# Seven steps moved in a hand-written order: two layers of graph network on one Trainium2 core

## The chip, the cores and the metric

The kernel runs on one core of one Trainium2 chip. The metric is the time of one execution on the device, in microseconds (us); less is better. A core has TensorE (PE, with its weight loads as a row of their own, PEld), VectorE (DVE), ScalarE (ACT), GpSimd (POOL) and SyncE (SP). Each has its own queue of instructions and they wait for each other on semaphores. In this kernel ACT, SP and POOL also issue the transfers.

## The reference

x holds 128 samples of 128 nodes with 512 features, adj is one 128x128 matrix for all samples. Two layers follow each other, each with its residual:

```python
h = jnp.maximum(_layernorm(x, axis=-1), 0.0)
x = x + _L0_gnn_ref(h, adj, Wq, Wk, Wv)      # layer 0
h = jnp.maximum(_layernorm(x, axis=-1), 0.0)
x = x + _L1_gnn_ref(h, adj, Wq, bq, Wk, bk, Wv, bv)   # layer 1
```

Layer 0 has no softmax. With q, k, v = h Wq^T, h Wk^T, h Wv^T it computes

```python
rel = adjacency.T[None, :, :] * (q @ k.T)
rel = rel / jnp.linalg.norm(rel, axis=2, keepdims=True)
out = rel @ v
```

Layer 1 is attention with 8 heads of 64: scores q k^T / 8, minus 1e9 where adj is 0, softmax over the last axis, times v. Everything is float32.

## The kernel before

The samples go through in 32 groups of four. Layer 0 of a group is an object `m`, layer 1 of the group before it `l`, layer 1 of the one before that `p`. The layer 1 that is being prepared for the next cycle is `n`, the layer 0 that is being prepared is `f`. A cycle of the loop runs a list of steps, `name.step` or `name.product.step`, in the order in which a string lists them (L657 to L689): FIRST in cycle 0, SECOND in cycle 1, ORDER in cycles 2 to 31, LAST at the end. The last cycle of ORDER has no `f`, and steps of a missing object are left out. The order holds for each engine: what a step gives to DVE stands in DVE's queue in the order of the list, and so for PE, ACT, POOL and SP. Between engines only data and buffers make anyone wait.

Big products (512x512 by 512 features) are made by a scheme with seven half-size products in place of eight: class `Product`, steps P1 P2 P5 P6 P3 P7 P4 in that order of issue. Each step is eight matmuls of 128x256 on PE (L229) into a PSUM bank. There are three banks to a product: x is used by P1, P6, P7, P4, which add onto it in turn, y by P2, z by P5 and P3. In between, a copy of the bank is kept (`keep`, an ACT copy, but for V of layer 1 a DVE addition with the bias, L246), and a later step's bank is added to the kept copy on DVE (L253). So P6 may write x only after P1's copy has read it, P7 after P6's copy, and P4 after P7's addition. Four banks are shared by all products (`ps_mm`). The products are G and V in layer 0 (tile names pg and pv), Q, K and V in layer 1 (pq, pk, pv). P5 and P6 read sums of the turned input, made by `sumA` and `sumB` (two DVE additions each).

The steps around the change:

- `stat b`, `inv i`: mean and variance of sample b on DVE (L294, L295); for samples 2i and 2i+1 rstd and shift on POOL (four small operations, L301 to L304).
- `hn i`, `rd i`, `T i`: normalisation and relu of two samples on ACT (L312), which then sends them to DRAM (d_h); SP fetches them in four blocks in another layout (u_h); DVE turns 32x32 blocks (L324). T0 gives the half x11, x12 of the input, T1 the half x21, x22. The tile `u` has two buffers, shared with `wr`.
- `R`, `mask_rel`, `square`, `N`, `norms`: layer 0's q k^T (32 matmuls, L393, bank pr), masked on DVE (L402), squared on ACT, summed on PE (L420) and taken to the power -1/2 on POOL.
- `O b`, `xO b`: rel times v on PE (L433), the residual on DVE (L439). O2 and O3 read what P4 of V gave.
- `S b`, `mk`/`mkA`/`mkB`/`add_mask`/`mx`: layer 1's scores (L471), mask and maximum on DVE.
- `ex`/`exC`/`exD`, `wr b`, `wt b`: the exponentials on ACT, sent to DRAM (d_w); SP's fetch (u_w); `wt` takes the reciprocal of the sums (L508) and turns the exponentials on DVE (L510).
- `A i`, `oc i`, `rdo i`, `ot i`: weights times v, and the way out.
- `start`: makes the tiles and products, and issues nothing.
- `w.sumk`, `w.sumq`: four additions each on the weights, on DVE.

S of sample 1 takes its two PSUM banks from `ps_o` (two buffers), which also holds pr of R and the results of O and A. The four fetch issues of `rd`, `wr` and `rdo` stand in SP's queue in the order of the list.

Of the kernel before, what the change touches and what calls it, by code (L numbers as in the profile page):

```python
# [21 lines left out]
def kernel(  # L22
# [354 lines left out]
    class Layer0(Layer):  # L377
        n = 0
# [62 lines left out]
    class Layer1(Layer):  # L441
        n = 1
# [215 lines left out]
        m.sumA m.sumB m.start f.stat0 f.stat1 f.inv0 m.G.P1 m.G.P2 f.stat2 f.stat3 f.inv1 w.sumw m.G.P5 f.hn0 f.rd0 m.G.P6  # L658
        w.scale m.G.P3 m.V.P1 f.hn1 f.rd1 w.sumv w.loadx m.G.P7 m.V.P2 w.sumq m.G.P4 m.V.P5
        m.R m.mask_rel m.square f.T0 m.V.P6 m.V.P3 m.N m.norms m.V.P7 m.O0 m.xO0 m.O1 m.xO1 n.stat0 n.stat1  # L660
        n.inv0 m.V.P4 n.hn0 n.rd0 f.T1 m.O2 m.xO2 m.O3 m.xO3 n.stat2 n.stat3 n.inv1 f.sumA f.start f.G.P1
        f.G.P2 f.sumB w.sumk f.G.P5 n.hn1 n.rd1 f.G.P6 f.G.P3 f.G.P7 n.T0 f.G.P4 n.T1 n.start
    """.split()
    SECOND = """
        l.Q.P1 l.sumA l.Q.P2 l.sumB l.K.P1 l.K.P2 l.Q.P5 l.Q.P6 f.load0 f.load1 l.Q.P3 l.K.P5 l.K.P6 l.Q.P7
        l.K.P3 l.K.P7 l.S0 l.mk0 f.load2 f.load3 l.Q.P4 l.K.P4 l.ex0 l.wr0 m.V.P1 f.stat0 f.stat1 f.inv0
        m.V.P2 m.V.P5 l.wt0 m.R m.mask_rel m.square f.stat2 f.stat3 f.inv1 m.V.P6 l.S1 m.N l.S2 l.mkA1 m.norms l.exC1
        l.mkB1 l.exD1 l.wr1 m.V.P3 l.add_mask2 m.V.P7 l.mx2 l.exC2 m.O0 m.xO0 m.O1 m.xO1 n.stat0 n.stat1 n.inv0
        m.V.P4 l.exD2 l.wr2 n.hn0 n.rd0 l.start_v l.V.P1 m.O2 m.xO2 m.O3 m.xO3 n.stat2 n.stat3 n.inv1 l.V.P2 l.V.P5
        l.wt1 n.hn1 l.V.P6 l.wt2  # L670
        n.rd1 l.V.P3 l.V.P7 n.T0 l.S3 l.A0 l.mk3 l.oc0 l.V.P4 l.ex3 n.T1 n.start
# [6 lines left out]
        l.wt0 f.load2 f.load3 m.R m.mask_rel m.square m.V.P6 l.S1 m.N l.S2 l.mkA1 m.norms l.exC1 l.mkB1 l.exD1  # L678
        l.wr1 m.V.P3 l.add_mask2 m.V.P7 l.mx2 l.exC2 m.O0 m.xO0 m.O1 m.xO1 n.stat0 n.stat1 n.inv0 m.V.P4 l.exD2
        l.wr2 n.hn0 n.rd0 l.start_v f.stat2 l.V.P1 m.O2 m.xO2 m.O3 m.xO3 n.stat2 n.stat3 n.inv1 l.V.P2 l.V.P5 l.wt1  # L680
        f.stat3 f.inv1 n.hn1 l.V.P6 l.wt2
        n.rd1 l.V.P3 l.V.P7 n.T0 l.S3 l.A0 l.mk3 l.oc0 l.V.P4 l.ex3 n.T1 n.start
    """.split()
    LAST = """
# [19 lines left out]
    with tc.manual_schedule(engines={EN.PE, EN.SP, EN.Pool, EN.DVE, EN.Activation}):  # L704
        p, l, m = None, None, Layer0(0)
# [9 lines left out]
        f = Layer0(1)  # L715
# [3 lines left out]
        for g in range(NG):  # L719
            n = Layer1(g)  # L720
            if g:
                f = Layer0(g + 1) if g + 1 < NG else None
            run((FIRST, SECOND, ORDER)[min(g, 2)], p=p, l=l, m=m, n=n, f=f, w=Weights1())
            p, l, m = l, n, f
# [31 lines left out]
```

## Time and profile before

| | |
|---|---|
| median of 3 runs | 2506.55 us (2505.88 to 2507.48) |
| the profiled execution | 2507.47 us, span of its instructions 2505.7 us |
| mean granted TensorE clock | 0.998 |
| one ordinary cycle, from R to R | 76.73 us in most |
| POOL busy | 531.5 us (21%) |
| transfers | 405.72 MB, mean 162 GB/s |

A page of the profile gives busy time for each engine and the chain of work that ended last. Finer views used below: the timeline, one row for a run of equal instructions (start, duration, engine, line, operation, output<-inputs, shape, count) with, in brackets, how long the engine was idle before it and who released it; the sums over stretches (windows); and the waits by who waited for whom. Starts are counted from the first instruction. The end of a matmul is modelled, so distances are taken from start to start.

### The profile page before, as it was taken

The page shows a single profiled execution, that of the slowest core. Times are in us where ns is not written, and L with a number is a line of the kernel's source. Part 1 is how long each engine was busy: PE and PEld are TensorE (multiplying, and loading weights), DVE is VectorE, ACT ScalarE, POOL GpSimd, SP SyncE. Part 2 cuts the span into 40 slices and gives each one's busy share as a digit, 9 for nine tenths or more (in the row PEclk, how much of TensorE's full clock was granted, in tenths as well). Part 3 has the DMA queues.
Part 4 walks back from the last instruction along what each step waited for, and adds up shares of the span by engine and source line. Part 5 has one row for each costly group of instructions (what it writes and reads, how often), then busy time and mean ns, then how long its engine had stood idle before and what let it go on. Part 6 is the DMA issues. An engine that isn't in the chain of part 4 may idle for free.

```text
span 2505.7 us, 40908 instructions
## 1 busy us (share of the span) xinstructions
PE 2488.6 (99%) x14688; PEld 2114.5 (84%) x14688; DVE 1716.3 (68%) x2547; ACT 1024.3 (41%) x3248; POOL 531.5 (21%) x944
## 2 busy tenths in 40 slices
PE   9999999999999999999999999999999999999998
PEld 7788888888888888888888888888888888888887
DVE  6467766667766677666677666776667776667766
ACT  3334434344434444343434344443434443444433
POOL 5011212212221212122121211221221212112211
PEclk9999999999999999999999999999999999999999
DMA  6155644555544555455564455554455644455543
GB/s 207 60 169 168 189 142 156 162 177 177 161 153 153 178 164 190 139 159 169 168 185 156 155 152 179 166 184 145 151 169 169 193 147 153 155 177 177 166 137 118
DMA packets 370476, 405.72 MB, mean 162 GB/s; under 512 B 29601, under 2 KB 286753, under 8 KB 370273
## 3 DMA queue, kind: packets, MB, share of 16 engines
q1 hardware_dynamic: 279520, 168.97, 25.3%
q10 hardware_dynamic: 69856, 165.70, 17.6%
q0 software_dynamic: 20896, 68.44, 8.3%
q8 instruction: 116, 1.90, 0.3%
q14 instruction: 88, 0.71, 0.1%
HBM read 204.80 MB, written 198.18 MB: 161 GB/s over the span
## 4 chain that ended last, share of the span: by engine, by line
PE 95%; DMA 2%; DVE 1%; ACT 1%; issue 0%; SPq 0%; POOL 0%; ACTq 0%; DVEq 0%; POOLq 0%
PE pv_x L229 17%; PE pg_x L229 9%; PE pv_z L229 9%; PE pk_x L229 8%; PE pq_x L229 8%; PE pg_z L229 5%; PE pq_z L229 4%; PE po L616 4%; PE pr L393 4%; PE pk_z L229 4%; PE po L433 4%; PE pv_y L229 4%; PE pss L471 4%; PE pg_y L229 2%; PE pk_y L229 2%; PE pq_y L229 2%
## 5 line engine op out<-in xcount | busy, mean ns | idle before, releaser
L651 POOL TENSOR_TENSOR xb<-xb,o 128x512 f32<-128x512 f32 x124 | 158.0, 1274 | 1205.6 <-DVE o L644 1204.1
L229 PE MATMUL pv_x<-wc_v,h 128*128 128x256 f32 x1280 | 303.8, 384 | 0.0
L229 PEld LDWEIGHTS pv_x<-wc_v,h 128*128 128x128 f32 x1280 | 238.0, 190 | 58.6 <-issue 20.8
L229 PE MATMUL pv_z<-wc_v,s 128*128 128x256 f32 x1024 | 245.9, 383 | 0.0
L312 ACT ACTIVATE hn<-xb,shift,rstd 128x512 f32<-128x512 f32 x252 | 191.0, 807 | 127.0 <-POOL shift L304 124.8
L324 DVE STREAM_TRANSPOSE h<-u_h 128x1024 f32<-128x1024 f32 x126 | 156.1, 1239 | 107.1 <-DMA u_h<-d_h 106.9
L229 PEld LDWEIGHTS pv_z<-wc_v,s 128*128 128x128 f32 x1024 | 192.6, 190 | 28.9 <-issue 0.2
L495 ACT ACTIVATE e<-pss,nmax 128x128 f32<-128x128 f32 x512 | 179.9, 381 | 89.5 <-DVE nmax L488 75.0
L627 ACT COPY oT<-po 128x512 f32<-128x512 f32 x124 | 72.6, 586 | 274.1 <-PE po L616 274.1
L229 PE MATMUL pq_x<-h,wc_q 128*128 128x256 f32 x768 | 181.8, 380 | 0.9 <-DVE h L324 0.8
L229 PE MATMUL pv_x<-wc_v,s 128*128 128x256 f32 x768 | 181.7, 379 | 0.0
L229 PE MATMUL pk_x<-h,wc_k 128*128 128x256 f32 x768 | 181.5, 379 | 0.0
L294 DVE BATCH_NORM_STATS2 st<-xb 128x6 f32<-128x512 f32 x256 | 170.8, 667 | 8.4 <-DMA xb<-in_x_dram 8.4
L510 DVE STREAM_TRANSPOSE wT<-u_w 128x1024 f32<-128x1024 f32 x126 | 153.4, 1218 | 21.0 <-DMA u_w<-d_w 18.4
L229 PEld LDWEIGHTS pq_x<-h,wc_q 128*128 128x128 f32 x768 | 145.4, 190 | 22.1 <-PE pv_x L229 2.0
L229 PEld LDWEIGHTS pk_x<-h,wc_k 128*128 128x128 f32 x768 | 145.8, 190 | 19.9
L229 PEld LDWEIGHTS pv_x<-wc_v,s 128*128 128x128 f32 x768 | 143.3, 190 | 18.4 <-issue 0.2
L644 DVE TENSOR_TENSOR o<-o,rs 128x512 f32<-128x512 f32 x124 | 124.4, 1003 | 4.3
L229 PE MATMUL pg_z<-s,wc_a 128*128 128x256 f32 x512 | 124.1, 385 | 0.0
L301 POOL TENSOR_SCALAR rstd<-mv 128x2 f32<-128x2 f32 x128 | 28.4, 222 | 447.5 <-DVE mv L295 445.2
L616 PE MATMUL po<-wT,v 128*64 128x128 f32 x1984 | 122.0, 276 | 0.0
L229 PE MATMUL pq_z<-s,wc_q 128*128 128x256 f32 x512 | 121.6, 380 | 0.3
(157 smaller groups left out, 4834.5 us busy)
## 6 DMA issues: line engine op xcount, KB each, us to landing
d_h<-hn ACTq DMA_DIRECT2D x126, 512.0 KB, 3.6
u_h<-d_h SPq DMA_DIRECT2D x504, 128.0 KB, 3.5
d_w<-e ACTq DMA_DIRECT2D x126, 512.0 KB, 2.7
u_w<-d_w SPq DMA_DIRECT2D x504, 128.0 KB, 3.2
xb<-in_x_dram POOLq DMA_DIRECT2D x124, 256.0 KB, 3.1
d_o<-oT ACTq DMA_DIRECT2D x62, 512.0 KB, 3.0
u_o<-d_o SPq DMA_DIRECT2D x248, 128.0 KB, 2.9
out_dram<-xb POOLq DMA_DIRECT2D x124, 256.0 KB, 3.0
```

Of the source, the lines that this page charges most:

```text
L229: nc.tensor.matmul(ps[:, m, :], lhsT=lhsT, rhs=rhs, start=first and m == 0 and k == 0, stop=k == 1, skip_group_check=True,)
L294: nc.vector.bn_stats(st, x_tiles[g, b])
L312: nc.scalar.activation(hn[:, r], x_tiles[g, b].rearrange("p (k j q) -> p j k q", j=TB, q=BK), AF.Relu, bias=self.shift[:, b : b + 1], scal ...
L324: nc.vector.transpose(half.rearrange("p k (t i) -> p t k i", i=BK), self.u.pop(i).rearrange("p t (k q) -> p t k q", q=BK),)
L393: nc.tensor.matmul(pr[:, b, :], lhsT=self.turned(k, b), rhs=self.gT[:, k, ts(b, P)], start=(k == 0), stop=(k == KD - 1),)
L433: nc.tensor.matmul(po, lhsT=self.rel[:, b, :], rhs=self.v[:, b, :], start=True, stop=True)
L471: nc.tensor.matmul(half[r][:, k, :], lhsT=self.qT[rows, k, ts(b, P)], rhs=self.kT[rows, k, ts(b, P)], start=True, stop=True,)
L495: nc.scalar.activation(e[:, :, i, :], sc[:, i, :].rearrange("p (j q) -> p j q", q=BK), AF.Exp, bias=nmax[:, i : i + 1], accum_out=self.tot ...
L510: nc.vector.transpose(self.wT[b].rearrange("p h (t i) -> p t h i", i=BK), self.uw.pop(b).rearrange("p t (h q) -> p t h q", q=BK),)
L616: nc.tensor.matmul(po[r * HD : (r + 1) * HD, k, :], lhsT=self.v[:, b, ts(2 * k + r, HD)], rhs=wT[:, r * NH + k, :], start=True, stop=True,)
L644: nc.vector.tensor_tensor(heads, heads, self.rs.pop(b).rearrange("p (r k) -> p k r", r=2)[:, :, :, None].to_broadcast([P, NH, 2, HD]), ALU ...
L651: nc.gpsimd.tensor_tensor(xb, xb, o.rearrange("p k t q -> p (k t q)"), ALU.add)
```

## The change

Only the strings of the order are edited. No instruction is added or removed, and no function is touched.

```diff
     FIRST = """
...
-        n.inv0 m.V.P4 n.hn0 n.rd0 f.T1 m.O2 m.xO2 m.O3 m.xO3 n.stat2 n.stat3 n.inv1 f.sumA f.start f.G.P1
-        f.G.P2 f.sumB w.sumk f.G.P5 n.hn1 n.rd1 f.G.P6 f.G.P3 f.G.P7 n.T0 f.G.P4 n.T1 n.start
+        n.inv0 m.V.P4 n.hn0 n.rd0 f.T1 f.start f.G.P1 f.sumA m.O2 m.xO2 m.O3 m.xO3 n.stat2 n.stat3 n.inv1
+        f.G.P2 f.sumB f.G.P5 n.hn1 n.rd1 f.G.P6 f.G.P3 n.T0 n.start f.G.P7 n.Q.P1 w.sumk f.G.P4 n.T1
     """.split()
     SECOND = """
-        l.Q.P1 l.sumA l.Q.P2 l.sumB l.K.P1 l.K.P2 l.Q.P5 l.Q.P6 f.load0 f.load1 l.Q.P3 l.K.P5 l.K.P6 l.Q.P7
+        l.sumA l.Q.P2 l.sumB l.K.P1 l.K.P2 l.Q.P5 l.Q.P6 f.load0 f.load1 l.Q.P3 l.K.P5 l.K.P6 l.Q.P7
...
-        m.V.P2 m.V.P5 l.wt0 m.R m.mask_rel m.square f.stat2 f.stat3 f.inv1 m.V.P6 l.S1 m.N l.S2 l.mkA1 m.norms l.exC1
-        l.mkB1 l.exD1 l.wr1 m.V.P3 l.add_mask2 m.V.P7 l.mx2 l.exC2 m.O0 m.xO0 m.O1 m.xO1 n.stat0 n.stat1 n.inv0
+        m.V.P2 m.V.P5 m.R m.mask_rel m.square f.stat2 f.stat3 f.inv1 m.V.P6 l.S1 m.N l.S2 l.mkA1 m.norms l.exC1
+        l.mkB1 l.exD1 l.wr1 l.wt0 m.V.P3 l.add_mask2 m.V.P7 l.mx2 l.exC2 m.O0 m.xO0 m.O1 m.xO1 n.stat0 n.stat1 n.inv0
...
     ORDER = """
...
-        f.stat3 f.inv1 n.hn1 l.V.P6 l.wt2
+        n.hn1 l.V.P6 f.stat3 f.inv1 l.wt2
```

In the first group `f.G.P1` and `f.sumA` go ahead of O2 and xO2, `w.sumk` goes from ahead of `f.G.P5` to behind `f.G.P7`, `n.T0` goes ahead of `f.G.P7`, and Q.P1 of the next group, until now the first step of SECOND, goes between `f.G.P7` and `f.G.P4`. In the second group `l.wt0` goes from ahead of R to behind the exponentials of sample 1. In the cycles of ORDER `f.stat3` and `f.inv1` go behind `l.V.P6`.

## The prediction, made before the change was run

> **What bounds the kernel now.** I read the page first, then the PE timeline, then whoever ends each of its waits.
>
> ```profile
> PE 2488.6 (99%) x14688; PEld 2114.5 (84%) x14688; DVE 1716.3 (68%) x2547; ACT 1024.3 (41%) x3248; POOL 531.5 (21%) x944
> PE 95%; DMA 2%; DVE 1%; ACT 1%; issue 0%; SPq 0%; POOL 0%; ACTq 0%; DVEq 0%; POOLq 0%
> ```
>
> TensorE sets the end: the change removes no matmul, so it can only win what PE waits. The PE timeline of the first two groups names those waits in brackets (start, duration, both us):
>
> ```profile
> 53.31 1.98 PE L433 MATMUL po<-v,rel 128*128 128x512 f32 x4 [0.68 <-ACT v L237]
> 66.43 1.99 PE L229 MATMUL pg_x<-h,wc_a 128*128 128x256 f32 x8 [0.78 <-DVE gT L253]
> ```
>
> ```profile
> 108.53 2.07 PE L471 MATMUL pso<-kT,qT 64*128 64x128 f32 x14 [3.74 <-DVE rel L402]
> 110.53 0.65 PE L420 MATMUL pv_y<-sq,ones 128*32 128x128 f32 x8
> 111.11 2.08 PE L471 MATMUL pss<-kT,qT 64*128 64x128 f32 x16
> 113.13 2.78 PE L229 MATMUL pv_z<-wc_v,s 128*128 128x256 f32 x8
> 138.57 1.96 PE L229 MATMUL pq_x<-h,wc_q 128*128 128x256 f32 x8 [0.50 <-DVE h L324]
> 190.43 1.16 PE L471 MATMUL pss<-kT,qT 64*128 64x128 f32 x16
> ```
>
> The pss product takes 2.08 after the long wait and 1.16 a group later: the wait costs more than its 3.74. The windows view says why; its column before the DMA share is the granted clock:
>
> ```profile
> 109.00:113.00 4.00, 4.00 (x38) 3.29 (x36) 3.71 (x9) 1.87 (x9) 2.37 (x5) 0.50 0.00 0
> ```
>
> Who holds rel (DVE timeline):
>
> ```profile
> 106.65 1.25 DVE L510 STREAM_TRANSPOSE wT<-u_w 128x1024 f32<-128x1024 f32 x1 [7.27 <-DMA u_w<-d_w]
> 107.82 0.65 DVE L402 TENSOR_TENSOR rel<-pr,adj_sb 128x512 f32<-128x512 f32 x1
> ```
>
> l.wt0 waits for a transfer, and m.mask_rel, whose input pr was complete at about 102.6, stands behind it. S1 needs the PSUM buffer that pr leaves.
>
> In the ordinary cycles there is a small wait. The PE page hides it (under 0.1 us); the weight loads (PEld) and DVE show it. The first fence below is cycle 3 with f.stat3 ahead of V.P6's copy, the second the last cycle, which has no f:
>
> ```profile
> 284.19 0.65 DVE L294 BATCH_NORM_STATS2 st<-xb 128x6 f32<-128x512 f32 x1
> 284.97 0.66 DVE L246 TENSOR_TENSOR pv_r<-pv_x,bv_sb 128x512 f32<-128x512 f32 x1
> 285.69 1.59 PEld L229 LDWEIGHTS pv_x<-wc_v,h 128*128 128x128 f32 x8 [0.32 <-DVE pv_r L246]
> ```
>
> ```profile
> 2435.35 0.65 DVE L246 TENSOR_TENSOR pv_r<-pv_x,bv_sb 128x512 f32<-128x512 f32 x1
> 2436.55 1.70 PEld L229 LDWEIGHTS pv_x<-wc_v,h 128*128 128x128 f32 x8
> ```
>
> **What the Trainium skill says.** "TensorE: Matmul & The Clock Gate", Part 1, "What's actually happening": after an idle window of about 3.4 us the array's clock falls to half. The trace agrees: 3.74 idle, then clock 0.50; after 0.68 and 0.78 no such drop. The same page, "Architectural detail", calls ACT and DVE strict FIFO: agreed, by rel behind wT. "SBUF — State Buffer", "Who interferes with whom": a VectorE operation with two SBUF inputs keeps GpSimd from reading SBUF. Agreed: the same POOL operation L301 takes 0.23 at 53.40 and 0.56 at 57.78, under f.sumA.
>
> **The change part by part.** A product step of 8 matmuls runs 1.727 from start to start (24.18 to 25.91 and so on), 1.82 ahead of or 1.83 behind one of other shape or after a wait; a wait therefore costs its length plus 0.10.
>
> *Second group, wt0 behind exD1.* Removed: DVE's wait. mask_rel then starts when pr ends (102.65), S1 finds its buffer at 103.3 and starts at 104.30 without a wait. Before, S1, N, S2 and V.P3 took from 104.30 to 115.74, 11.44; the same four in cycle 3 take 1.092+0.356+1.092+1.831=4.37. Gain 7.07. Late next: wt0 (0.11+1.12) now stands just ahead of V.P3's add. In cycle 3 DVE is idle 0.48 there, so that add moves from 10.03 to 10.70 after R's start and ends at 11.37, O0 is due at 11.49. I charge 0.1 (bounds 0 and 0.2). Its transfer landed at 106.53, 7.6 after R's start; wt0 comes at 9.6: covered by 2.0. exC2, V.P4's copy and hn0 follow 0.66 later; O2 had 0.94 of slack to V.P4's copy. Of SP's queue, wr2 finds the u buffer that wt0 leaves at 11.0 before it is due (19.9).
>
> *The fetch behind it.* From V1.P4 to Q.P5 of the third group PE lost 0.74+0.32=1.06 waiting for T0 and T1 (u_h). T0 started 31.2 after R less the 7.07, against 29.5 to 31.15 in the ordinary cycles; only five of those 29 waited, 2.6 us together. rd0 stays gated by wt1 (u has two buffers). hn0's 0.66 eats part, so I take 0.5 off (bounds 0 and 1.06).
>
> *First group.* G.P1 (1.73) goes ahead of O2/O3, which wait for V.P4's copy: the wait of 0.84+0.10=0.94 is gone. Q.P1 between G.P7 and G.P4 covers P7's add: 0.95+0.10=1.05 gone. Both together would bring Q.P2 from 69.99 to 68.02. But ACT keeps n.hn1 ahead of G.P6's copy, and G.P7 may write its bank only after that copy. hn1 hangs on O3, stat2, stat3, inv1. DVE: T1 at 53.33, now sumA (1.30) ahead of xO2, so POOL's inv1 starts at 57.78+1.30=59.08. Its four operations took 3.07, all under two-SBUF-input work, and take 1.62 undisturbed (53.40 to 55.02); now sumB covers a part: 2.4, to 61.5. hn1 at 61.5; from hn1's start to the copy's end it was 2.54 (60.99 to 63.53), so 64.07. G.P7 was due at 62.83: a new wait of about 1.3 plus 0.1. Then P3's add and T0 (0.61+1.23) end at 65.95, u_h from hn0 (landed 63.89; sumA's lock on inv0 may add 0.6) is in time, Q.P1 starts at 66.1, G.P4 at 67.9, Q.P2 at 69.7. Gain 0.3. Bounds: inv1 undisturbed, 1.1 (T0 binds then); inv1 at 3.07, −0.3. w.sumk (2.7 of DVE) moves behind P7's add and ends near 69.5, K.P5 uses it after 80. sumA, T1, Q.P2's add stay in order; f.start and n.start issue nothing on an engine.
>
> *One statistic later, 29 cycles.* stat3 (0.78 with its aggregate) behind V.P6's copy. PE loses 0.079 before P7 and 0.104 in it, 0.183, alike in all 29 cycles with an f. The last cycle shows the new order: copy at 23.87 after R instead of 24.65, no wait. P7 needs it 0.32 earlier, it comes 0.78 earlier. The two only swap, so wt2 behind them stays where it was; inv1 on POOL ends 0.6 later, near 287.3 in cycle 3, and hn1 of the next cycle reads it at 303.7. Late next is T0: Q.P1 then comes 0.18 sooner. T0's end lies 0.65 to 1.4 ahead of it in 24 cycles (0.15 is the least possible); in the other five the fetch takes the gain. 24×0.183=4.4 (bounds 3.8 and 5.3).
>
> **Sum.** −7.0 −0.5 −0.3 −4.4 = −12.2. The profiled execution took 2507.47 (span 2505.7 and 1.8 around it): 2495.3. It lay 0.9 above the median of the runs, 2506.55, from which it would be 2494.35; I take 2494.8.
>
> **The rivals.**
> 1. *The last edit gives nothing*, because every cycle then waits for T0 instead. For it: five cycles do. Against: the slack of the other 24. 2494.8+4.4=2499.2.
> 2. *wt0's transfer takes the removed wait's place*: O0 waits for V.P3's add behind wt0, over 3.4 us with the half clock. For it: d_w took 4.5 here, 2.7 in the median. Against: 2.0 of cover. 7.0 lost: 2501.8, inside the bound of no change.
> 3. *Slower*: the fetch of u_h into T0 becomes the bound of all cycles, because PE's earlier steps put d_h and u_h on top of other transfers. Place: T0's wait ahead of Q.P1 and Q.P5. Price: the worst cycle lost 0.83; 29×0.83−2.6=21.5, the last edit and the fetch give nothing (4.9): 2494.8+26.4=2521.2. It outweighs the rest from some 0.34 a cycle (7.3+2.6 over 29), that is if u_h lands over a microsecond later than now. Against: hn0, hn1 and rd0 keep their times after R in these cycles.
>
> That PE's waits aren't removed as ordered (each engine keeps its own order) I give no share of its own: it is within the case bounds.
>
> **How the numbers follow.** Forecast 0.87, rival 1 0.06, rival 2 0.03, rival 3 0.04. The bounds add to gains from 10.4 to 14.5: from 2506.55−14.5 to 2507.47−10.4, 2492.0 to 2497.1; with transfers that vary by about a microsecond, 2491.8 to 2498.2. 0.2% is 5.0 us, about what a measurement can tell from no change: faster 0.93, same 0.03, slower 0.04.
>
> **What would show it.** No wait at pso in the second group and clock 1.00 there; a wait of about 1.1 shown at the second pg_x of G (P7), released by ACT's pg_r, none at O2 or G.P4; PEld pv_x without its wait on pv_r in 29 cycles; R to R 76.55 instead of 76.73 in most cycles. A wait at O0 or T0 waits in most cycles would prove me wrong.

## The result and the profile after

| | before | after |
|---|---|---|
| median | 2506.55 us (2505.88 to 2507.48, 5 runs) | 2495.74 us (2495.21 to 2497.27, 5 runs) |
| profiled execution | 2507.47, span 2505.7 | 2495.21, span 2493.4 |

The ratio is 0.996, with a 95% interval from 0.9949 to 0.9971: faster by 0.43% (10.8 us between the medians, 12.3 between the profiled executions). The measured time lies in the range, 0.9 us above the predicted one.

The page of the kernel after still shows TensorE as the bound. Its busy time fell by 8.7 us: about 3.3 are the slow matmuls behind the long wait (7.07 less the 3.74 idle), and about 5.3 are the small waits of the ordinary cycles, which the page had counted as busy because ends of matmuls are modelled.

```profile
PE 2479.9 (99%) x14688; PEld 2116.8 (85%) x14688; DVE 1715.5 (69%) x2547; ACT 1024.6 (41%) x3248; POOL 530.8 (21%) x944
PE 96%; DVE 1%; DMA 1%; ACT 1%; issue 0%; SPq 0%; POOL 0%; ACTq 0%; DVEq 0%; POOLq 0%
```

The PE timeline of the first two groups after (start, duration, what, and in brackets the idle time before it):

```profile
54.16 1.88 PE L433 MATMUL po<-v,rel 128*128 128x512 f32 x4
...
63.70 1.99 PE L229 MATMUL pg_x<-s,wc_a 128*128 128x256 f32 x8 [0.76 <-ACT pg_r L237]
65.64 1.97 PE L229 MATMUL pq_x<-h,wc_q 128*128 128x256 f32 x8
67.44 1.89 PE L229 MATMUL pg_x<-h,wc_a 128*128 128x256 f32 x8
...
103.48 1.16 PE L471 MATMUL pso<-kT,qT 64*128 64x128 f32 x16
104.57 0.43 PE L420 MATMUL pv_y<-sq,ones 128*32 128x128 f32 x8
104.93 1.16 PE L471 MATMUL pss<-kT,qT 64*128 64x128 f32 x16
```

O2/O3 (po) and G.P4 (the last pg_x) have no bracket any more. G.P7 at 63.70 has a new one, released by ACT's copy, as forecast. pso starts without a wait, and pss takes 1.16 instead of 2.08. The windows view over that place shows the full clock (1.00, third figure from the right; before the change it was 0.50 behind the wait):

```profile
101.00:105.00 4.00, 4.00 (x42) 3.20 (x40) 2.57 (x6) 1.22 (x2) 0.67 (x2) 1.00 0.47 129
```

mask_rel (L402) now waits for its own input, the product pr, and for nothing else (DVE timeline of the second group):

```profile
101.86 0.69 DVE L402 TENSOR_TENSOR rel<-pr,adj_sb 128x512 f32<-128x512 f32 x1 [3.40 <-PE pr L393]
```

An ordinary cycle, number 3, in the timelines of DVE and of the weight loads: V.P6's copy comes right behind wt1, the statistic behind it, and P7's weights load without a bracket.

```profile
275.50 0.65 DVE L246 TENSOR_TENSOR pv_r<-pv_x,bv_sb 128x512 f32<-128x512 f32 x1
276.08 0.67 DVE L294 BATCH_NORM_STATS2 st<-xb 128x6 f32<-128x512 f32 x1
```

```profile
276.71 1.70 PEld L229 LDWEIGHTS pv_x<-wc_v,h 128*128 128x128 f32 x8
```

From R to R it is 76.55 us instead of 76.73 in 24 of the 29 cycles with an f. Where the time went, from the starts of PE's steps in both traces (each step's distance to the next, less what the same step takes without a wait):

| stretch | before | after | difference |
|---|---|---|---|
| up to R of group 0 | 39.72 | 39.69 | -0.03 |
| R of group 0 to R of group 1 | 59.19 | 58.40 | -0.79 |
| second group: lost from S1 to V.P3 | 7.07 | 0 | -7.07 |
| second group: lost at V.P4 and A0 | 0 | 0.16 | +0.16 |
| second group: lost ahead of Q.P1 and Q.P5 | 1.06 | 0.30 | -0.76 |
| 29 ordinary cycles: lost at P3 and P7 | 5.31 | 0 | -5.31 |
| 29 ordinary cycles: lost ahead of Q.P1 and Q.P5 | 2.62 | 4.19 | +1.57 |

The sum is -12.2, the difference of the spans -12.3.

### The profile page after: what moved, and what is told of

Its sections match the earlier page's. It is cut to its first block, busy times and chain, and to the rows that moved or that the text cites. A ratio compares the mean times of both kernels' runs of the same rounds, so it can differ in the third digit from the quotient of the medians.

```text
span 2493.4 us, 40879 instructions
## 1 busy us (share of the span) xinstructions
PE 2479.9 (99%) x14688; PEld 2116.8 (85%) x14688; DVE 1715.5 (69%) x2547; ACT 1024.6 (41%) x3248; POOL 530.8 (21%) x944
## 4 chain that ended last, share of the span: by engine, by line
PE 96%; DVE 1%; DMA 1%; ACT 1%; issue 0%; SPq 0%; POOL 0%; ACTq 0%; DVEq 0%; POOLq 0%
PE pv_x L229 17%; PE pv_z L229 9%; PE pg_x L229 9%; PE pq_x L229 9%; PE pk_x L229 9%; PE po L616 5%; PE pr L393 5%; PE pg_z L229 5%; PE pq_z L229 4%; PE pk_z L229 4%; PE pv_y L229 4%; PE po L433 4%; PE pss L471 4%; PE pg_y L229 2%; PE pk_y L229 2%; PE pq_y L229 2%
## 5 line engine op out<-in xcount | busy, mean ns | idle before, releaser
L324 DVE STREAM_TRANSPOSE h<-u_h 128x1024 f32<-128x1024 f32 x126 | 156.1, 1239 | 100.2 <-DMA u_h<-d_h 99.6
L229 PEld LDWEIGHTS pv_z<-wc_v,s 128*128 128x128 f32 x1024 | 192.3, 190 | 28.3
```

Of the source, the lines that this page charges most:

```text
L229: nc.tensor.matmul(ps[:, m, :], lhsT=lhsT, rhs=rhs, start=first and m == 0 and k == 0, stop=k == 1, skip_group_check=True,)
L324: nc.vector.transpose(half.rearrange("p k (t i) -> p t k i", i=BK), self.u.pop(i).rearrange("p t (k q) -> p t k q", q=BK),)
```

## The experiments

The theory: the three parts each take their own waits away and don't touch each other; what is left in the ordinary cycles is the wait for u_h ahead of T0. Rivals: one part does it all; the long wait costs only its idle time; in the ordinary cycles T0's wait takes all back. Waits below are counted from start to start, together with the slower steps right behind them.

### One part at a time

First group alone (FIRST as in the change, and `l.Q.P1` out of SECOND):

```diff
-        ... n.rd0 f.T1 m.O2 m.xO2 m.O3 m.xO3 n.stat2 n.stat3 n.inv1 f.sumA f.start f.G.P1
-        f.G.P2 f.sumB w.sumk f.G.P5 n.hn1 n.rd1 f.G.P6 f.G.P3 f.G.P7 n.T0 f.G.P4 n.T1 n.start
+        ... n.rd0 f.T1 f.start f.G.P1 f.sumA m.O2 m.xO2 m.O3 m.xO3 n.stat2 n.stat3 n.inv1
+        f.G.P2 f.sumB f.G.P5 n.hn1 n.rd1 f.G.P6 f.G.P3 n.T0 n.start f.G.P7 n.Q.P1 w.sumk f.G.P4 n.T1
```

> The kernel before with the first group's edit alone. The theory (each part takes its own PE waits and the parts don't touch each other) expects the first group to end its cycle 0.8 us earlier (R of group 0 to R of group 1 58.4 instead of 59.2), the long wait at pso with the half clock still there, 0.183 us lost in all 29 ordinary cycles, and about 0.8 us less in all, not to be told from no change. A rival in which the first group's edit is what removes the long wait expects 7 to 8 us.

Measured: 2505.02 us against 2505.73 for the kernel before beside it, ratio 0.9998 (0.9989 to 1.0006), no change that can be told. In the trace 58.41 from R of group 0 to R of group 1, the wait at pso is there, and so is the 0.183 in all 29 cycles. The wait at pso cost 5.3 here and not 7.1. The transfer landed 0.5 sooner after R, and the slow stretch behind the wait was shorter:

```profile
107.80 1.55 PE L471 MATMUL pso<-kT,qT 64*128 64x128 f32 x14 [3.25 <-DVE rel L402]
109.28 0.65 PE L420 MATMUL pv_y<-sq,ones 128*32 128x128 f32 x8
109.86 2.08 PE L471 MATMUL pss<-kT,qT 64*128 64x128 f32 x16
111.87 1.99 PE L229 MATMUL pv_z<-wc_v,s 128*128 128x256 f32 x8
```

Here the slow stretch lies elsewhere than before: pso runs at nearly full speed for part of its time, N and pss at half, and V.P3 (pv_z) at full speed again. The theory holds for this part by its trace, and the rival is out; the gain of 0.8 is too small for the medians to show it.

Second group alone:

```diff
-        m.V.P2 m.V.P5 l.wt0 m.R m.mask_rel ...
-        l.mkB1 l.exD1 l.wr1 m.V.P3 ...
+        m.V.P2 m.V.P5 m.R m.mask_rel ...
+        l.mkB1 l.exD1 l.wr1 l.wt0 m.V.P3 ...
```

> The kernel before with l.wt0 alone moved behind exD1 and wr1 in the second group. The theory expects no wait at pso, a clock of 1.00 there, S1 to V.P3 in about 4.4 us instead of 11.44, about 0.08 lost at O0, and 7.0 to 7.7 us less in all. A rival in which the cost of the wait is its 3.74 us alone expects 3.7.

Measured: 2499.86 us, ratio 0.9977 (0.9969 to 0.9986), 5.9 us less. The wait at pso and the slow matmuls are gone, 7.07 as expected, 0.07 comes at the step ahead of V.P4:

```profile
103.73 1.16 PE L471 MATMUL pso<-kT,qT 64*128 64x128 f32 x16
104.83 0.43 PE L420 MATMUL pv_y<-sq,ones 128*32 128x128 f32 x8
105.18 1.16 PE L471 MATMUL pss<-kT,qT 64*128 64x128 f32 x16
```

In all it missed the expected 7.0 to 7.7. In this profile T0 and T1 of the third group made PE wait for 1.89, where it was 1.06 before, and the waits for u_h in the ordinary cycles came to 3.4 instead of 2.6. The trace puts the rival's 3.7 out, S1 to V.P3 having gone from 11.44 to 4.37: the idle time of 3.74 costs nearly twice itself. The medians alone would not, as their interval goes from 3.5 to 7.8.

The statistic alone:

```diff
-        f.stat3 f.inv1 n.hn1 l.V.P6 l.wt2
+        n.hn1 l.V.P6 f.stat3 f.inv1 l.wt2
```

> The kernel before with f.stat3 and f.inv1 alone moved behind V.P6. The theory expects the 0.183 us gone in all 29 ordinary cycles (5.3 us), part of it taken back by waits for u_h ahead of T0 in a handful of cycles, so 3.5 to 4.5 us less in all. The rival (all cycles wait for T0 instead) expects waits ahead of Q.P1 or Q.P5 in most cycles and about nothing less.

Measured: 2502.15 us (2499.86 to 2504.53), ratio 0.9985 (0.9978 to 0.9992), 3.6 us less. In the profile the 0.183 is gone in all 29 cycles; five of them wait for u_h, 2.4 us together. The rival asked for waits in most cycles. By their medians the three parts alone add to 0.7+5.9+3.6=10.2 us (the first of them can't be told from nothing); the whole was 10.8. That agrees within the noise, which is about 2 us for each part.

### What holds G.P7, and what is next

```diff
-        f.G.P2 f.sumB f.G.P5 n.hn1 n.rd1 f.G.P6 f.G.P3 n.T0 n.start f.G.P7 n.Q.P1 w.sumk f.G.P4 n.T1
+        f.G.P2 f.sumB f.G.P5 f.G.P6 n.hn1 n.rd1 f.G.P3 n.T0 n.start f.G.P7 n.Q.P1 w.sumk f.G.P4 n.T1
```

> The changed kernel with n.hn1 and n.rd1 behind f.G.P6 in the first group, so that ACT copies G's bank x first. If ACT's order is what holds G.P7, its wait (0.92 from start to start and 0.10 after it) is gone. The theory says that T0 is next: u_h landed at 64.2, so Q.P1 can't start before about 65.6 and gets a wait of about 1.1 in its place; the whole is then unchanged within 0.2 us. The rival (the copy was the only bound there) expects Q.P2 about 1.1 us earlier than 69.17.

Measured: 2495.33 us, the changed kernel having 2495.74 elsewhere; beside its own kernel before the ratio is 0.996 for both. The PE timeline, and DVE's of the same stretch:

```profile
63.07 1.89 PE L229 MATMUL pg_x<-s,wc_a 128*128 128x256 f32 x8
65.81 1.96 PE L229 MATMUL pq_x<-h,wc_q 128*128 128x256 f32 x8 [0.85 <-PE pg_x L229]
```

```profile
64.46 1.25 DVE L324 STREAM_TRANSPOSE h<-u_h 128x1024 f32<-128x1024 f32 x1 [0.43 <-DMA u_h<-d_h]
```

G.P7 has no wait, Q.P1 has it instead. The releaser in the bracket is the wrong one: pg_x of the step before is no input of Q.P1. T0 (L324) is, and it ended at 65.7. From R of group 0 to R of group 1 it is 58.28 against 58.40: ACT's order held G.P7, T0 is right behind it, and the rival's 1.1 us isn't there.

### Why the same few cycles wait for u_h

In the kernel after, the waits ahead of Q.P1 and Q.P5 stand in cycles 4, 9, 22 and 27 (1.29, 0.92, 0.51 and 1.36; 0.10 in cycle 24), nearly the cycles of before (4, 9, 22, 24 and 27). Two T0 of the profile after, of cycle 4 and of cycle 12:

```profile
359.61 1.25 DVE L324 STREAM_TRANSPOSE h<-u_h 128x1024 f32<-128x1024 f32 x1 [3.31 <-DMA u_h<-d_h]
```

```profile
972.46 1.25 DVE L324 STREAM_TRANSPOSE h<-u_h 128x1024 f32<-128x1024 f32 x1 [1.76 <-DMA u_h<-d_h]
```

After R that is 31.42 in cycle 4 and 29.67 in cycle 12. The last two of the four blocks of u_h landed 30.9 and 31.3 after R in cycle 4, and 29.0 and 29.5 in cycle 12. What four of the five waiting cycles share is a packet of queue q8, kind instruction. There are 116 of 16 KB in the whole profile, about one for 253 of PE's 29,376 matmuls and weight loads, so I take them for fetches of PE's own instructions. In cycle 4 one is under way while the last two blocks of u_h are (DMA view of a stretch of 1.4 us; it holds one of 16 engines for 1.3 us):

```profile
q1 hardware_dynamic: 118, 0.05, 24.3%
q8 instruction: 1, 0.02, 5.7%
```

To test it, the number of PE's instructions ahead of the cycles was changed: the 16 transposes at the start (L123) write a tile that nobody reads.

```diff
-        for _ in range(16):
+        for _ in range(0):
             nc.tensor.transpose(idle, ident, ident)
```

> The changed kernel without the 16 transposes into the tile idle at the start (32 of PE's instructions, no part of the result). It shifts where in the cycles PE's own instruction fetches fall (queue q8, 16 KB each, one per 256 of PE's instructions, some 21 us) by some 2.6 us to later. In the changed kernel the waits ahead of Q.P1 and Q.P5 stand in cycles 4, 9, 22 and 27, those in which such a fetch comes 27.6 to 28.3 us after R. The theory that the fetch is what makes u_h late expects these cycles free of waits, and waits, if any, in 14 and 19, whose fetches came at 24.3 and 24.8. The rival (the data of these groups, or the transfers' own timing) expects the waits in 4, 9, 22 and 27 as before. The start itself may lose or win a microsecond or two.

The same with `range(48)`:

> The changed kernel with 48 in place of 16 transposes into the tile idle at the start, no part of the result: 64 of PE's instructions more, so its instruction fetches fall some 5.2 us earlier in the cycles; the start is some 7 us longer. The theory that the fetch makes u_h late expects the waits ahead of Q.P1 and Q.P5 to leave cycles 4, 9, 22 and 27 and to stand in cycles whose fetch came at 32.9 to 33.7 before: 3, 5, 8, 13, 18, 23, 28, or some of these. The rival expects them in 4, 9, 22 and 27.

And with wide matmuls:

```diff
-        idle = ps_o.tile([P, P], F32, tag="po", name="idle")
-        for _ in range(16):
-            nc.tensor.transpose(idle, ident, ident)
+        idle = ps_o.tile([P, 4, P], F32, tag="po", name="idle")
+        for _ in range(4):
+            nc.tensor.matmul(
+                idle, lhsT=ident, rhs=ident[:, None, :].to_broadcast([P, 4, P]), start=True, stop=True,
+            )
```

> The changed kernel with four matmuls of 512 columns in place of 16 transposes of 128 into the tile idle at the start (no part of the result): about as long, but 16 of PE's instructions fewer, so PE's instruction fetches fall some 1.4 us later in the cycles. By the two shifts seen so far, waits ahead of Q.P1 come with a fetch at 27.0 to 28.3 us after R. The theory that the fetch makes u_h late expects those of cycles 4, 9, 22 and 27 at 29.0 to 29.7 and those of 14 and 19 at 25.7 and 26.2, so in the cycles from the third on at most two with a wait, under 1 us together where the changed kernel lost 4.2, and about 2492.5 in all. The rival (chance, or the transfers' own timing) expects 3 to 5 us of waits again and about 2495.5.

Beside it the changed kernel itself once more:

> The changed kernel unaltered, beside the one above on the same chip: 2495 to 2497, waits ahead of Q.P1 in cycles 4, 9, 22 and 27 as in its first profile if they hang on the place of the instruction fetches, in others if they are chance.

Measured in cycles 2 to 30 of each of the eleven profiles (the fetch's start after R; the waits ahead of Q.P1 and Q.P5 with what follows them; the last kernel is that of the next section):

| kernel | median | cycles with a fetch at 26.9 to 28.3, their waits | fetch at 28.31 to 29.2 | waits in other cycles |
|---|---|---|---|---|
| before | 2506.55 | 4, 9, 22, 27: 0.70, 0.32, 0.26, 0.83 | 2, 7, 12, 17: none | 24: 0.52 |
| first group alone | 2505.02 | 4, 9, 22, 27: 0.50, 0.49, 0.32, 0.33; 7: none | 12, 17: none | 24: 0.41 |
| second group alone | 2499.86 | 4, 27: 0.84, 0.83 | 9, 22: 0.75, 0.96; 7, 12, 17: none | none |
| after | 2495.74 | 4, 9, 22, 27: 1.29, 0.92, 0.51, 1.36 | 2, 7, 12, 17: none | 24: 0.10 |
| after again | 2496.32 | 4, 9, 22, 27: 1.44, 0.95, 0.59, 1.26 | 2, 7, 12, 17: none | 24: 0.03 |
| hn1 behind G.P6 | 2495.33 | 4, 9, 22, 27: 0.62, 1.29, 0.50, 0.75 | 2, 7, 12, 17: none | 24: 0.14 |
| statistic alone | 2502.15 | 9, 22, 27: 1.20, 0.46, 0.50 | 2, 7, 12, 17: none | 4, 24: 0.16, 0.07 |
| no transposes | 2498.89 | 9, 14, 19, 24, 29: 0.56, 0.61, 1.28, 1.02, 0.57 | 4, 22, 27: none | 11: 0.18 |
| 48 transposes | 2499.45 | 2, 10, 15, 20, 25, 30: 0.81, 0.58, 0.86, 0.34, 1.05, 0.72 | 5, 23, 28: none | none |
| wide matmuls | 2497.93 | 4, 9, 14, 19: 0.63, 0.83, 1.00, 0.99 | 7, 12, 17, 22, 27: none | none |
| sum of small edits | 2497.15 | 4, 9, 19, 27: 0.92, 0.69, 1.05, 0.32 | 7, 12, 17, 22: none | 14: 0.08 |

Without the transposes 4, 22 and 27 are free of waits and 14 and 19 have them, as the theory said. Cycle 9 kept one against the forecast (its fetch stood at 28.0), and 24 and 29 got one that nobody had named. With 48 the waits left 4, 9, 22 and 27 altogether, but stand in 2, 10, 15, 20, 25 and 30 and in none of the cycles that were named: the fetches of 5, 23 and 28 came at 28.5 to 28.8, just too late. The wide matmuls missed their aim. They were expected to bring at most two waits and under 1 us; the fetches of 4 and 9 didn't move by 1.4 but stood at 27.6 and 27.9, and four cycles lost 3.4 together, the amount that the rival had named. So where a fetch falls isn't set by the count of instructions alone, and the forecasts of single cycles failed in part.

What holds is a link, with exceptions. Of 45 cycles with a fetch at 26.9 to 28.3, 44 have a wait, of 0.3 to 1.4. Of 42 with a fetch at 28.31 to 29.2, two have one (0.75 and 0.96, second group alone). The three exceptions are all in kernels that still have the old order of the statistic. Nine cycles have a wait of 0.03 to 0.52 with no fetch in either place. Cycle 24 gives six of them, and there SP issued the fetch of the last block of u_h 1.3 to 1.5 later after R than in cycle 4 (26.6 to 26.9 against 25.3), so another cause is likely. The bounds were drawn from the profiles themselves. Only the kernel with wide matmuls and the last one were forecast with nearly the same ones (27.0 to 28.3), and they kept to them but for the 0.08.

The start variants also move everything by 2.4 to 2.8 us. But in the kernels with 48 transposes and with wide matmuls R of group 0 comes at the same time (42.48 and 42.46), and from there on the two have the same work; their waits stand in different cycles. So the data of the groups don't decide which cycles wait, and a fixed moment hardly does. Chance is out too, as the changed kernel run again has its waits where it had them. How one packet of 16 KB makes the last blocks of u_h land over a microsecond later stays open. So does the edge at 28.3: the start of a fetch is itself read among the packets of u_h, and a fetch that begins late may simply be one that found them done.

The three start variants are slower as a whole: 2497.93 to 2499.45 against 2496.32 for the changed kernel run again (its neighbour for the wide matmuls alone; the other two ran elsewhere). R of group 0 comes at 42.1 to 42.5 instead of 39.7. Without the transposes PE's first matmuls of 512 columns took 0.85 each instead of 0.43, and 48 transposes or four wide matmuls last 6.6 us instead of 3.5.

### A sum of small edits

The last kernel has hn1 behind G.P6, wt0 behind V.P3's addition, and eight transposes with one wide matmul at the start.

```diff
-        l.mkB1 l.exD1 l.wr1 l.wt0 m.V.P3 l.add_mask2 m.V.P7 l.mx2 l.exC2 ...
+        l.mkB1 l.exD1 l.wr1 m.V.P3 l.wt0 l.add_mask2 m.V.P7 l.mx2 l.exC2 ...
```

> The changed kernel with three small edits: n.hn1 and n.rd1 behind f.G.P6, l.wt0 behind V.P3's addition in the second group, and eight transposes and one matmul of 512 columns in place of the 16 transposes into the tile idle (no part of the result; about as long, 12 of PE's instructions fewer). Expected: the 0.075 at O0 gone, since that addition no longer stands behind wt0; the first group as with hn1 moved alone (R to R 58.28); and in cycles 2 to 30 waits ahead of Q.P1 in those cycles, and only those, whose instruction fetch comes 27.0 to 28.3 us after R, whichever they are: the three shifts so far did not land where a constant distance would have put them. The whole 2492 to 2496, by how many such cycles there are. The rival (the fetch has no part in it) expects waits in cycles with fetches elsewhere.

Measured: 2497.15 us (2493.71 to 2498.63), ratio to before 0.9964 (0.9951 to 0.9978), so no version that beats the changed kernel. The fetch's part held: fetches at 26.9 to 28.3 in 4, 9, 19 and 27, all four with waits of 0.3 to 1.1, four cycles with a fetch at 28.31 to 28.6 without one, and 0.08 in cycle 14. The edit of wt0 made it worse. The loss at this place, expected to go, grew from 0.08 to 0.60, and the weight loads say why, first in the changed kernel, then here:

```profile
111.21 0.78 PEld L229 LDWEIGHTS pv_x<-wc_v,h 128*128 128x128 f32 x4 [0.51 <-DVE v L253]
```

```profile
111.84 2.24 PEld L232 LDWEIGHTS pv_x<-wc_v,h 128*128 128x128 f32 x11 [1.16 <-DVE v L256]
```

This is V.P4, not O0. It may write bank x only after P7's addition has read it, and that addition comes later still when wt0 stands behind P3's (L253 and L256 are the same line of the source, three lines lower in the second kernel).

## Why the prediction was right

*Second group.* 7.07 was forecast and 7.07 measured, and the part alone shows that wt0's place does it. The windows at 109 to 113 and the slow pss had said that the wait costs its idle time and a stretch of half clock. "TensorE: Matmul & The Clock Gate", Part 1, "What's actually happening", gives about 3.4 us of idleness for that; after 3.74 the clock was 0.50, and with the first group alone after 3.25. These two are counted from modelled ends. From the start of the last matmul ahead of the wait to the start of the next it was 4.02 and 3.52, so the runs neither contradict the 3.4 nor fix it to a tenth. The Trainium skill's page calls its windows free-running, which fits the two slow stretches: with the first group alone pso began again at full speed (0.11 from one pair of matmuls to the next) and was slow only from 0.7 us on, before the change it was slow at once.

*The charge for wt0's new place.* I took 0.1 at O0. Measured 0.08, but at V.P4, behind P7's addition: I followed the addition that moved first and not the next one in DVE's queue, which moved as well. A0 lost another 0.08, as wt2 waited 2.21 for its transfer; this wasn't in the sum, and the same kernel run again didn't lose it.

*The fetch behind it.* 0.5 taken off, 0.76 measured, within the bounds. That it came so near is luck. The same kernel run again waited 0.90 there and not 0.30, a gain of 0.16, and the runs go from a gain of 1.06 (statistic alone) to a loss of 0.83 (second group alone). Here too the wait goes with a fetch of PE's instructions. In the five kernels with the second group's edit whose fetch came at 27.9 to 28.6 after R the wait was 0.90 to 1.89, and in the three whose fetch came at 20.8 or 33.7 it was 0 to 0.30.

*First group.* The mechanism was right in each step: both old waits gone, a new one at G.P7 released by ACT's copy behind hn1, T0 next. Its size was off: 0.3 forecast, 0.79 measured. The term is inv1 on POOL, put at 2.4:

```profile
59.02 0.22 POOL L301 TENSOR_SCALAR rstd<-mv 128x2 f32<-128x2 f32 x1 [3.69 <-DVE mv L295]
59.32 0.71 POOL L302 TENSOR_TENSOR rstd<-rstd,mhalf 128x2 f32<-128x2 f32 x1
60.10 0.70 POOL L303 TENSOR_SCALAR shift<-mv 128x2 f32<-128x2 f32 x1
60.88 0.20 POOL L304 TENSOR_TENSOR shift<-shift,rstd 128x2 f32<-128x2 f32 x1
```

That is 2.06, from 59.02 to 61.08. Of the four operations only L303, which began under the second of sumB's two additions, was held up (0.70 instead of 0.23). I had charged all of sumB's time at the slow rate of before; an operation under way when the addition began (L302, from 59.32; sumB from 59.43) kept its usual 0.71. "SBUF — State Buffer", "Who interferes with whom", says that issue order decides who blocks, and this fits. It also calls the shared port an exclusive lock; that the addition was then held up isn't seen here, as it began in its turn and took its usual 0.68. So hn1 started at 61.11 and not 61.5, G.P7's wait was 0.92+0.10 and not 1.4, and Q.P1 behind it lost 0.07, not 0.25.

*The statistic.* The 0.183 in 29 cycles is gone, 5.31 of 5.31, as the last cycle of before had shown. Taken back by T0: 1.57, where I had 0.9. I let the five cycles that already waited lose their 0.18 each. They lost more, as u_h landed later in three of them: in cycle 4 T0 started 31.42 after R where it had been 31.01. The step that failed in size is "in the other five the fetch takes the gain": the term was put at 4.4 with bounds of 3.8 and 5.3, and 3.74 was measured, just below them.

*The sum.* 12.2 was forecast, and the two profiled executions differ by 12.3. In part this is luck: the first group gave 0.49 more than its term and the fetch behind the second 0.26 more, wt0's place took 0.06 more and the statistic gave 0.66 less, which nearly cancel. Between the medians it is 10.8, because the profiled execution before lay 0.9 above its median and the one after 0.5 below.

*The rivals.* 1 (T0 takes all back) would need waits in most cycles; there are four or five. 2 (wt0's transfer late at O0): it was landed when wt0 came, as DVE's recip and wt0 followed mkB1 without a bracket. 3 (slower) is out with the result.

## What to carry to other kernels

On an engine that is 99% busy, time the steps from start to start against the same step elsewhere: that finds waits of 0.08 us that the page doesn't list, shows what a wait costs beyond its idle time, and a cycle that lacks the edited step shows what the edit will give. When a step is moved in an in-order queue, price every step behind it, not only its next neighbour: the one that hurts is the one that releases a buffer. If a transfer is late in the same few cycles of every run, look at what else moves data then, the instruction fetches included, before calling it chance; and count the link over every trace at hand, also those made for another question, as its exceptions may stand there.

## What the runs showed of the hardware

A DMA queue of kind instruction moves packets of 16 KB, 116 in a profile, one for about 253 of PE's matmuls and weight loads; each holds one of the 16 DMA engines for 0.9 to 1.9 us. When the number of PE's instructions at the start was changed, they fell elsewhere in the cycles. In the eleven profiles such a packet began 26.9 to 28.3 us after R in 45 cycles, while u_h was under way, and in 44 of them PE waited 0.3 to 1.4 us for u_h; of 42 cycles with the packet just later two had a wait. Why the blocks land so much later isn't shown.

PE's first matmuls run at half speed: 128x128 transposes took 0.213 from start to start at the start and 0.109 at 15.5 us. Without these transposes the first six matmuls of 512 columns took 0.85 or more, and the later ones 0.43.

A wait in mid-stream cost PE more than its length: 3.74 us idle cost 7.07, and 3.25 cost 5.3, with the clock at 0.50 behind both; 0.76 idle (0.92 from start to start) cost 1.02, with no such drop.
